# Copies and row scalings of layers 1 to 3 choose ScalarE or VectorE when the list scheduler places them

## The chip, the core and the metric

The kernel runs on one core of a Trainium2 chip. A core has five engines that run at the same time, each with its own in-order queue of instructions: TensorE (PE in the profile; its weight loads are a row of their own, PEld), VectorE (DVE), ScalarE (ACT), GpSimd (POOL) and SyncE (SP, which here issues the DMAs). They wait for each other through semaphores. Matrix products land in PSUM, a small memory of eight banks per core; GpSimd takes no part in reading it here, so whatever leaves PSUM is read by VectorE or ScalarE. The main memory on the chip is SBUF, 128 partitions wide.

The metric is the time of one execution in microseconds (us) on the device, as a median over runs.

## What is computed

Four layers in a row, with five attentions between them, over 32 sequences of 64 tokens with 256 features, and a context tensor of the same shape. All in fp32. Cut to its core:

```
x = x + Wo0 @ attn(norm(x), ctx)          # layer 0: 8 heads of 64, over channels
a = layernorm(ctx) * g + b                # layer 1: 16 heads of 16
x = x + tanh(gate) * attn(x Wq, a Wk, a Wv, mask) Wo
h = concat(ctx, x)                        # layer 2: queries from x, 128 keys
o = attn(x Wq, h Wk, h Wv, mask) Wo + x
x = x + gelu(rmsnorm(o) W1) W2            # with biases; hidden size 1024
x = x + attn(layernorm(x), itself) Wo     # layer 3, self-attention, mask applied to the scores
x = x + attn(layernorm(x), ctx) Wo        # layer 3, cross-attention
x = x + gelu(layernorm(x) W1) W2          # layer 3, MLP of 1024
```

"Layers 1 to 3" are all but the first, which holds an attention without the split into small heads. The code counts the attentions of layers 1 to 3 as `l` = 0 to 3: layer 1, layer 2, and the two of layer 3.

## The kernel before

**Tiling.** The 32 sequences make eight groups of four. A group's tokens are a tile of 128 partitions x 2 x 256 values (`xs[g]`). Attention goes in units: each unit is a pair of sequences with 16 heads of 64 keys (layer 2 takes two units a pair, with 8 heads of 128 keys each). The scores of a unit, 128 x 1024, fill one PSUM buffer (`s4`, a single one for the whole core). A unit then goes: maximum (DVE), subtraction (DVE, or POOL for every second masked unit), exponential (ACT), sum and reciprocal (DVE), scaling by POOL or a spread of the reciprocals to a row (`a_rows`, tile `rx`), two times four transposes on PE with a copy out of PSUM each (`a_turn`, tile `PTe`), 64-column products with the values (`a_values`), and a copy of the result (`a_fin`).

**Split precision.** Projections run as fp32r products of a high and a low part: `to_fm` transposes a tile, copies it to a rounded high part (`xTh...`), and subtracts that from the source for the low part (`xTl...`). So almost every projection waits for a copy and then for a subtraction. The same is done for the MLP's hidden tile (`u` to `xThh` and `xTlh`).

**Copies.** The operations that this case is about are these: the row scaling of the layer norms (`ln_apply`; its result is a tile in `boot`, scaled and shifted by two [128,1] columns `rstd` and `nmr`), the high part in `to_fm`, the evictions of queries and keys (`put`, tiles `qfm` and `kfm`, with or without a bias column), the values scattered into their places (`v_out`, `vbd`), `rx`, `PTe`, the attention result (`a_fin`: `rb`, `xTho`), the high part of the context (`split_`, `xTh<-boot`), and the high part of the MLP's hidden tile (`xThh<-u`). In the kernel before, all of them run on ScalarE, save a few value scatters on VectorE. The source lies in PSUM for most of them; `boot`, `rx`, `xTh<-boot`, `xThh` and `xTho<-rb` go from SBUF to SBUF.

**What sets the order.** Layer 0 (the first 440 us) is written out by hand; the weights' loading and the prologue of layer 1 are held in chains from which `fill` slips operations in. From `plan.on = True` (L1592) on, nothing is issued directly: every operation is recorded with a due time, and `Plan.go` (L246) orders the whole of layers 1 to 3. `link` finds the dependences from tiles and byte ranges; two engines in one PSUM bank are kept in order. `order` (L289) is a list scheduler: with a modelled time for each operation (`cost`, L194) it takes, again and again, the ready operation that can start earliest, on the engine that it is recorded for; among equals it takes the most urgent, by due time, less 3 for what drains PSUM, plus a random tie-breaker of up to 0.5 drawn from `SEED`. Each engine's queue then holds its instructions in just that order, and the slots of all tiles are chosen there too. All recorded operations carry one line in the profile, L125 (`write`); those of layer 0 carry L156 (`call`).

In `cost`, VectorE's time for a copy or a scaling from SBUF is 0.3 + 1.05e-3 us a column, from PSUM 0.14 + 1.05e-3; ScalarE's is 0.115 + 0.92e-3, 0.03 more from SBUF and 0.105 more for each [128,1] operand.

Of the kernel before, what the change touches and what calls it, by code (L numbers as in the profile page):

```python
# [20 lines left out]
D = 256  # L21
# [72 lines left out]
class Plan:  # L94
# [2 lines left out]


    RING = {"pj": 40}
    SEED, TIE = 4, 0.5  # L100

    def __init__(self, engines):
        self.engines = engines
# [12 lines left out]
    def shape(self, shape, dt):  # L116
        if self.scratch is None:
            import concourse.bacc as bacc
            self.scratch = bacc.Bacc("TRN2", target_bir_lowering=False, num_devices=1)
        self.n += 1  # L120
        return self.scratch.dram_tensor(f"s{self.n}", tuple(shape), dt, kind="ExternalInput").ap()

    def write(self, o):
        real = lambda x: x.real() if isinstance(x, View) else x
# [68 lines left out]

    def cost(self, o):  # L194

        outs, ins = o.outs, o.ins
        width = lambda x: max(1, self.size(x))
        w = width(outs[0])
        if o.key == "T":
            if o.method == "transpose":  # L200
                return 0.11, 0.25, (1, 1)
            l, r = ins[0], ins[1]
            k_, m_ = l.shape[0], self.size(l)
            rows = 4 if k_ <= 32 else 2 if k_ <= 64 else 1
            cols = 4 if m_ <= 32 else 2 if m_ <= 64 else 1
            n_ = self.size(r)
            if l.dtype == F32:
                return max(n_ * 1.67e-3, 0.1 if rows * cols == 1 else 0) / (rows * cols), 0.3, (rows, cols)
            return max(n_ * 0.418e-3, 0.12 if rows * cols == 1 else 0) / (rows * cols), 0.25, (rows, cols)
        if o.key == "S":  # L210
            return 0.64, 2.0, None
        w = max([w] + [width(x) for x in ins])
        out_of_banks = any(isinstance(x, View) and x.root.psum for x in ins)
        if o.key == "V":
            if o.method == "reciprocal":
                return 0.14 + w * 7e-3, 0.05, None
            if w <= 16:
                return 0.2, 0.05, None
            if out_of_banks or o.method in ("tensor_reduce", "bn_stats"):
                return 0.14 + w * 1.05e-3, 0.05, None  # L220
            return 0.3 + w * (1.05e-3 if o.method in ("tensor_copy", "tensor_scalar") else 1.3e-3), 0.05, None
        if o.key == "A":
            gelu = any(x == AF.Gelu_apprx_tanh for x in o.p)
            exp = any(x == AF.Exp or x == AF.Square for x in o.p)
            t = 0.115 + w * 0.92e-3 + 0.105 * len([x for n, x in o.k.items() if n in ("bias", "scale") and self.is_ap(x)])
            return t + (0 if out_of_banks or exp else 0.03), 0.1, "gelu" if gelu else "exp" if exp else None
        if o.method == "memset":
            return 0.1 + w * 0.85e-3, 0.05, None
        if w <= 16:
            return 0.75 if any(x == ALU.pow for x in o.p) else 0.3, 0.05, None  # L230
        three = len([x for x in ins if width(x) > 1]) > 1
        return 0.1 + w * (2.45e-3 if three and not self.repeats(ins[1]) else 1.95e-3), 0.05, None
# [21 lines left out]
    def link(self):  # L254
        atoms, seen = [], {}
        for i, o in enumerate(self.ops):
# [16 lines left out]
            for (name, rt, p0, p1, f0, f1), writes in places:  # L273
                if rt is not None and rt not in at.roots:
                    at.roots.append(rt)
                acc = seen.setdefault(name, [])
                for b, q0, q1, g0, g1, w in acc:
                    if b is at:
                        continue
                    bank = rt is not None and rt.psum and b.key != at.key  # L280
                    if bank or ((writes or w) and p0 < q1 and q0 < p1 and f0 < g1 and g0 < f1):
                        at.before[b] = True
                        b.after[at] = True
                if writes:
                    acc[:] = [x for x in acc if not (p0 <= x[1] and x[2] <= p1 and f0 <= x[3] and x[4] <= f1 and x[0] is not at and not (rt is not None and rt.psum))]
                acc.append((at, p0, p1, f0, f1, writes))
        return atoms

    def order(self, atoms):  # L289
# [25 lines left out]
        for at in atoms:  # L315
            at.wait = len(at.before)
            at.at = 0.0
            at.urgent = at.due + ties.uniform(0, self.TIE) - (3.0 if at.key in "VA" and any(isinstance(x, View) and x.root.psum for o in at.ops for x in o.ins) else 0.0)
            if not at.wait:
                ready[at.key].append(at)  # L320
        out = []

        def slots(at):
# [23 lines left out]
        while len(out) < n:  # L347
            best = None
            for e, rs in ready.items():
                cand = []  # L350
                for at in rs:
                    s = slots(at)
                    if s is None:
                        continue
                    t = max(free[e], at.at, s)
                    if at.form is not None and e == "A" and form.get(e) not in (None, at.form):
                        t += 0.4
                    cand.append((t, at))
                if not cand:
                    continue  # L360
                t0 = min(t for t, _ in cand)
                t, at = min(((t, at) for t, at in cand if t <= t0), key=lambda x: (x[1].urgent, x[1].index))
                if best is None or t < best[0]:
                    best = (t, at)
            if best is None:
                stuck = [(k, at.due, at.ops[0].method, [r.slot for r in at.takes]) for k, rs in ready.items() for at in rs]
                raise RuntimeError(f"no order: {len(out)} of {n}, {stuck[:20]}")
            t, at = best
            e = at.key
            ready[e].remove(at)  # L370
            d = at.time
            if at.form is not None:
                if form.get(e) not in (None, at.form):
                    d += 0.12 if e == "T" else 0.0
                    if e == "A":
                        t += 0.9
                form[e] = at.form
# [19 lines left out]
            for b in at.after:  # L397
                b.wait -= 1
                b.at = max(b.at, (t + d if b.key == e else end) + 0.06 * (b.key != e))
                if not b.wait:  # L400
                    ready[b.key].append(b)
            at.written = True
            out.append(at)
        self.atoms = out
# [4 lines left out]
def mk_kernel(ctx: ExitStack, tc: tile.TileContext, a: dict, out: bass.AP):  # L409
# [489 lines left out]
    def ln_apply(x, mv, rstd, tag):  # L899
        z = wt([P, 2, D], F32, "z", 2)  # L900
        nmr = wt([P, 2], F32, "nmr" + tag, 2)
        for i in range(2):
            G.tensor_scalar(nmr[:, i:i + 1], mv[:, i, 0:1], rstd[:, i:i + 1], -1.0, ALU.mult, ALU.mult)
            A.activation(z[:, i], x[:, i], AF.Identity, bias=nmr[:, i:i + 1], scale=rstd[:, i:i + 1])
        return z

    def to_fm(x, tag=""):
# [4 lines left out]
                T.transpose(p_[:, k * D + i * P:k * D + (i + 1) * P], x[:, i, k * P:(k + 1) * P], ident)  # L912
        hi, lo = fm_tiles(tag)
        hf, lf = hi.rearrange("p k t -> p (k t)"), lo.rearrange("p k t -> p (k t)")
        A.copy(hf, p_)
        V.tensor_tensor(lf, p_, f32(hf), ALU.subtract)
        return (hi, lo)

# [28 lines left out]
        return o  # L947

    def put(d, s_, bias):
        if bias is None:  # L950
            A.copy(d, s_)
        else:
            A.activation(d, s_, AF.Identity, bias=bias)

    def k_out(w, x, bias):

# [8 lines left out]
    def v_out(w, x, vb, vl, part=None):  # L965
# [3 lines left out]
        for b in range(2):  # L969
            for e in range(2):  # L970
# [3 lines left out]
                else:  # L974
                    dst = vb[e][part * 64:(part + 1) * 64]
                dst = dst.rearrange("p (i b) h d -> p i b h d", b=2)[:, :, b, :, e * 16:(e + 1) * 16]
                if vl == 1 and b == 0 and e == 0 or cur["boot"] and e == 0:
                    V.tensor_copy(dst, src)
                else:
                    A.copy(dst, src)  # L980

    def kbd_make(kt, kbs_, part=None):

# [75 lines left out]
    def a_rows(u):  # L1059
        u["rx"] = []  # L1060
        if u["kind"] != "k":
            rx = wt([P, 16, 16], F32, "rx", 2)
            sm = u["sm"].rearrange("p (r c h) -> p r c h", r=4, c=2).unsqueeze(4).broadcast_to([P, 4, 2, 2, 16])
            A.copy(rx.rearrange("p (c r h) d -> p r c h d", c=2, r=4), sm)
            rx = rx.rearrange("p (c h) d -> p c (h d)", c=2)
            u["rx"] = [rx[:, 0], rx[:, 1]]

    def a_turn(u, c):
# [1 line left out]
        for r in range(4):  # L1070
            T.transpose(pt[:, r * P:(r + 1) * P], u["e"][:, r, c * P:(c + 1) * P], ident)
        pe = wt([P, 4, P], F32, "PTe", 4)
        A.copy(pe.rearrange("p h q -> p (h q)"), pt)
        u.setdefault("pt", []).append(pe)

    def a_values(u):
# [12 lines left out]
    def a_fin(u):  # L1089
# [5 lines left out]
        hv, lv = [t[:, c, i * P:(i + 1) * P] for t in st["o"]]  # L1095
        ov = o_[:, 0:D].rearrange("p (c t) -> p c t", c=2)[:, c]
        if u["kind"] == "k":
            A.copy(hv, ov)
            V.tensor_tensor(lv, ov, f32(hv), ALU.subtract)
        else:  # L1100
            rb = wt([P, 2, P], F32, "rb", 2)
            A.copy(rb.rearrange("p c t -> p (c t)"), o_[:, D:2 * D])
            V.tensor_tensor(rb, ov, rb, ALU.mult)
            A.copy(hv, rb)
            G.tensor_tensor(lv, rb, f32(hv), ALU.subtract)

    def out_add(w, x, resid, dst):
# [121 lines left out]
    def ctx_steps(l, g, due, src=()):  # L1229
# [6 lines left out]

        def split_():
            hi, lo = fm_tiles()
            A.copy(hi, st["raw"])
            G.tensor_tensor(lo, st["raw"], f32(hi), ALU.subtract)  # L1240
            st["c"] = (hi, lo)
        step(n + "a", due - 2, fetch, *src)
# [36 lines left out]
    def mlp_steps(l, g, w, b1, row, key, dues, out_=None):  # L1279
# [3 lines left out]
        def up(j):  # L1283
# [7 lines left out]
                A.activation(t[:, c], p_[:, c * D:(c + 1) * D], AF.Gelu_apprx_tanh, bias=b1[:, j * 2 + c:j * 2 + c + 1])  # L1291
            st[f"h{j}"] = fm_tiles("h")
            hh, hl = st[f"h{j}"]
            A.copy(hh, t)
            V.tensor_tensor(hl, t, f32(hh), ALU.subtract)

        def down(j):
# [372 lines left out]
```

## Time and profile before

| | us |
|---|---|
| median of 3 runs | 1141.58 (1139.43 to 1143.37) |
| the profiled execution | 1139.34 |
| its span, first to last instruction | 1137.6 |
| PE busy in the span | 1064.6 |
| ACT busy | 909.2 |
| DVE busy | 861.2 |
| POOL busy | 783.1 |

A busy share is an average over stages that have different limits, so the stages are read one by one: layer 0 to about 440 us, a passage of some 25 us to the scheduled part, then layers 1, 2 and 3 in turn, overlapping by group. Idle time of an engine costs time only where another engine that sets the end waits for it. The span of a matrix instruction in the profile is modelled and overlaps with its neighbours, so that PE counts as busy somewhat beyond what it must do.

### The profile page before, as it was taken

What the parts mean: (1) busy time and instruction counts of PE and PEld (TensorE: products, weight loads), DVE (VectorE), ACT (ScalarE), POOL (GpSimd) and SP (SyncE); (2) the same over time, 40 slices, a digit from 0 to 9 for tenths busy, and PEclk for the clock granted to TensorE, in tenths of its full rate; (3) what the DMA queues carried; (4) which work ended last, traced back from release to release, by engine and by line L of the source; (5) the groups of instructions that cost most, each with busy time, mean ns of one, the idle gap of its engine ahead of it and who ended that gap; (6) DMA issues with size and microseconds to landing.
All of it is one profiled execution on the core that took longest, in us unless ns stands there. A gap on an engine that the chain in (4) does not pass through costs nothing.

```text
span 1137.6 us, 35727 instructions
## 1 busy us (share of the span) xinstructions
PE 1064.6 (94%) x14396; PEld 872.7 (77%) x14396; DVE 861.2 (76%) x1485; ACT 909.2 (80%) x2326; POOL 783.1 (69%) x919
## 2 busy tenths in 40 slices
PE   6999999999999996699999999999999989889998
PEld 4666666666666664588988989998998868779998
DVE  3778888787888872678788977777878888777842
ACT  2888888888888984477778888889898787878974
POOL 3789888888888864546545554457866999996520
PEclk9999999999999998799999999999999998989999
DMA  3001111111011000211211100001000111110000
GB/s 96 20 24 39 41 38 34 34 34 35 27 37 33 26 20 29 88 49 39 79 51 44 36 27 28 22 11 39 21 20 20 48 51 51 42 33 22 11 20 29
DMA packets 41301, 41.22 MB, mean 36 GB/s; under 512 B 7059, under 2 KB 37796, under 8 KB 41136
## 3 DMA queue, kind: packets, MB, share of 16 engines
q1 hardware_dynamic: 40816, 38.54, 10.9%
q8 instruction: 114, 1.87, 0.7%
q10 hardware_dynamic: 320, 0.40, 0.1%
q14 instruction: 51, 0.42, 0.1%
HBM read 26.30 MB, written 2.10 MB: 25 GB/s over the span
## 4 chain that ended last, share of the span: by engine, by line
PE 42%; POOL 8%; DVE 5%; ACT 2%; issue 1%; DVEq 0%; POOLq 0%; ACTq 0%
PE pj L125 39%; PE s L125 4%; POOL E L125 3%; DVE E L125 2%; DVE mx L125 1%; POOL xTlo L125 1%; POOL xTl L125 1%; ACT PTe L125 1%; DVE sm L125 1%; POOL boot L125 1%; POOL w L125 1%; POOL x L125 1%; POOL wraw L125 0%; ACT L125 0%; POOL rstda L125 0%
## 5 line engine op out<-in xcount | busy, mean ns | idle before, releaser
L156 POOL TENSOR_TENSOR E<-E,rs 128x512 f32<-128x512 f32 x256 | 263.2, 1042 | 51.7 <-DVE rs L156 46.7
L156 ACT ACTIVATE E<-sc,mx 128x256 f32<-128x256 f32 x512 | 237.9, 479 | 11.8 <-DVE rs L156 11.1
L156 DVE TENSOR_REDUCE mx<-sc 128x4 f32<-128x1024 f32 x128 | 156.3, 1221 | 6.6 <-PE sc L156 2.6
L156 PE MATMUL sc<-cd,T 64*128 64x256 f32 x1024 | 143.7, 400 | 11.7 <-ACT E L156 11.1
L125 POOL TENSOR_TENSOR E<-E,sm 128x512 f32<-128x512 f32 x96 | 101.2, 1079 | 68.5 <-DVE sm L125 55.8
L156 PE MATMUL av<-PT,us 128*64 128x256 f32 x1024 | 125.2, 385 | 0.3 <-DVE PT L156 0.3
L156 PEld LDWEIGHTS av<-PT,us 128*64 128x64 f32 x1024 | 68.1, 136 | 60.3 <-issue 21.0
L156 PEld LDWEIGHTS pt<-ident,E 64*128 64x128 f32 x2048 | 83.3, 139 | 37.4 <-POOL E L156 20.1
L156 PEld LDWEIGHTS sc<-cd,T 64*128 64x128 f32 x1024 | 89.2, 189 | 27.7 <-ACT E L156 19.8
L125 DVE TENSOR_REDUCE sm<-E 128x16 f32<-128x1024 f32 (+1 forms) x80 | 96.0, 1200 | 16.1 <-ACT E L125 16.0
L156 ACT ACTIVATION_READ_ACCUMULATOR E<-sc,mx 128x1 f32 x512 | 106.7, 208 | 0.0
L125 ACT COPY PTe<-pj 128x512 f32<-128x512 f32 x160 | 88.0, 590 | 17.7 <-PE pj L125 15.6
L125 PE MATMUL pj<-ident,E 128*128 128x128 f32 x640 | 90.3, 279 | 9.0 <-ACT E L125 3.2
L156 PE MATMUL pt<-ident,E 64*128 64x64 f32 x2048 | 94.7, 227 | 3.3 <-ACT PT L156 1.0
L125 PE MATMUL pj<-w,xThh 128*128 128x256 f32 x512 | 93.4, 287 | 0.1
L156 DVE COPY PT<-pt 128x512 f32<-128x512 f32 x128 | 86.7, 678 | 8.5 <-PE pt L156 7.8
L156 ACT COPY PT<-pt 128x512 f32<-128x512 f32 x128 | 75.3, 588 | 22.2 <-PE pt L156 21.0
L125 PE MATMUL pj<-xThn,w 128*128 128x256 f32 x512 | 92.3, 286 | 0.7 <-DVE rb L125 0.4
L156 DVE RECIPROCAL rs<-sm 128x2 f32<-128x2 f32 x256 | 40.7, 159 | 64.3 <-ACT E L156 60.1
L125 ACT ACTIVATE E<-E 128x1024 f32<-128x1024 f32 x80 | 84.9, 1062 | 5.4 <-DVE E L125 4.2
L125 PEld LDWEIGHTS pj<-ident,E 128*128 128x128 f32 x640 | 71.0, 142 | 17.7 <-ACT E L125 3.7
L125 DVE TENSOR_TENSOR xTlh<-u,xThh 128x512 fp32r<-128x512 f32 x64 | 54.2, 850 | 30.5 <-ACT xThh L125 30.2
(229 smaller groups left out, 2782.5 us busy)
## 6 DMA issues: line engine op xcount, KB each, us to landing
kb<-kfm SPq DMA_DIRECT2D x44, 128.0 KB, 2.0
xd<-in_x SPq DMA_DIRECT2D x32, 128.0 KB, 2.9
cd<-in_ctx SPq DMA_DIRECT2D x32, 128.0 KB, 2.7
boot<-in_ctxT SPq DMA_DIRECT2D x16, 256.0 KB, 2.9
kb<-kfm SPq DMA_DIRECT2D x64, 64.0 KB, 1.9
xt<-in_x SPq DMA_DIRECT2D x16, 128.0 KB, 2.0
boot<-in_ctx SPq DMA_DIRECT2D x8, 256.0 KB, 2.7
out<-x SPq DMA_DIRECT2D x8, 256.0 KB, 2.1
```

Source lines behind the costliest of these rows:

```text
L125: getattr(self.engines[o.key], o.method)(*[real(x) for x in o.p], **{k: real(x) for k, x in o.k.items()})
L156: return f(*p, **k)
```

## The change

A new method `Plan.either` records a copy, or a scaling by columns, under a key "F" instead of an engine. It holds two forms: an ACTIVATE for ScalarE (function Copy, or Identity with bias and scale) and a copy or a tensor-scalar instruction for VectorE. In `order` such an operation stands in the ready lists of both engines. VectorE may take it only where it could start there at least `WORTH` = 0.5 us sooner than on ScalarE by the scheduler's own times. When it is placed, it becomes that engine's form. Outside the scheduled part (the prologue) it always goes to ScalarE. ScalarE's form was a copy instruction before, and is an ACTIVATE with the function Copy after. Two "F" operations in one PSUM bank are kept in order of recording. The fixed rule that sent some value scatters of layer 2 to VectorE is gone, the one for the prologue stays. `SEED`, which draws the tie-breakers, goes from 4 to 3.

```diff
-    SEED, TIE = 4, 0.5
+    SEED, TIE = 3, 0.5
+    WORTH = 0.5
...
+    def either(self, d, src, bias=None, scale=1.0):
+
+        o = Op()
+        o.key, o.due, o.extra = "F", self.due, self.extra
+        self.extra = []
+        if bias is None:
+            o.method, o.p, o.k = "activation", (d, src, AF.Copy), dict(scale=scale)
+            o.other = ("tensor_copy", (d, src)) if scale == 1.0 else ("tensor_scalar", (d, src, scale, None, ALU.mult))
+        else:
+            o.method, o.p, o.k = "activation", (d, src, AF.Identity), dict(bias=bias, scale=scale)
+            o.other = ("tensor_scalar", (d, src, bias, None, ALU.add)) if isinstance(scale, float) else ("tensor_scalar", (d, src, scale, bias, ALU.mult, ALU.add))
+            assert not isinstance(scale, float) or scale == 1.0
+        if self.on:
+            self.ops.append(o)
+            return
+        o.key = "A"
...
@@ link
-                    bank = rt is not None and rt.psum and b.key != at.key
+                    bank = rt is not None and rt.psum and (b.key != at.key or at.key == "F")
@@ order
-                ready[at.key].append(at)
+                for e in "AV" if at.key == "F" else at.key:
+                    ready[e].append(at)
...
                     t = max(free[e], at.at, s)
+                    if at.key == "F" and e == "V" and max(free["A"], at.at, s) < t + self.WORTH:
+                        continue
...
+            if at.key == "F":
+                o = at.ops[0]
+                if e == "V":
+                    d = o.on_v
+                    o.method, o.p, o.k = *o.other, {}
+                o.key = e
...
@@ ln_apply
-            A.activation(z[:, i], x[:, i], AF.Identity, bias=nmr[:, i:i + 1], scale=rstd[:, i:i + 1])
+            plan.either(z[:, i], x[:, i], nmr[:, i:i + 1], rstd[:, i:i + 1])
@@ to_fm
-        A.copy(hf, p_)
+        plan.either(hf, p_)
@@ put
-        if bias is None:
-            A.copy(d, s_)
-        else:
-            A.activation(d, s_, AF.Identity, bias=bias)
+        plan.either(d, s_, bias)
@@ v_out
-                if vl == 1 and b == 0 and e == 0 or cur["boot"] and e == 0:
+                if cur["boot"] and e == 0:
                     V.tensor_copy(dst, src)
                 else:
-                    A.copy(dst, src)
+                    plan.either(dst, src)
@@ a_turn
-        A.copy(pe.rearrange("p h q -> p (h q)"), pt)
+        plan.either(pe.rearrange("p h q -> p (h q)"), pt)
@@ up (MLP)
-            A.copy(hh, t)
+            plan.either(hh, t)
...
```

The copies of `a_rows` (`rx`), of `a_fin` (`rb`, `xTho`) and of `split_` (`xTh<-boot`) are replaced in the same way.

More of the change, by code (lines that the diff above doesn't have):

```diff
@@ L121, in shape @@
         return self.scratch.dram_tensor(f"s{self.n}", tuple(shape), dt, kind="ExternalInput").ap()
+    def either(self, d, src, bias=None, scale=1.0):
[13 more added lines that the diff above has]
+        o.key = "A"
+        if self.chain is not None:
+            self.chain.append(o)
+        else:
+            self.write(o)
     def write(self, o):
@@ L194, in cost @@
     def cost(self, o):
+        if o.key == "F":
+            o.key = "V"
+            m, p, k = o.method, o.p, o.k
+            o.method, o.p, o.k = o.other[0], o.other[1], {}
+            o.on_v = self.cost(o)[0]
+            o.key, o.method, o.p, o.k = "A", m, p, k
+            t = self.cost(o)
+            o.key = "F"
+            return t
         outs, ins = o.outs, o.ins
@@ L317, in order @@
             at.at = 0.0
-            at.urgent = at.due + ties.uniform(0, self.TIE) - (3.0 if at.key in "VA" and any(isinstance(x, View) and x.root.psum for o in at.ops for x in o.ins) else 0.0)
+            at.urgent = at.due + ties.uniform(0, self.TIE) - (3.0 if at.key in "VAF" and any(isinstance(x, View) and x.root.psum for o in at.ops for x in o.ins) else 0.0)
             if not at.wait:
-                ready[at.key].append(at)
+                for e in "AV" if at.key == "F" else at.key:
+                    ready[e].append(at)
         out = []
@@ L364, in order @@
                     best = (t, at)
+                    at.engine = e
             if best is None:
@@ L368, in order @@
             t, at = best
-            e = at.key
-            ready[e].remove(at)
+            e = at.engine
+            for q in "AV" if at.key == "F" else at.key:
+                ready[q].remove(at)
             d = at.time
+            if at.key == "F":
[4 more added lines that the diff above has]
+                o.key = e
             if at.form is not None:
@@ L400, in order @@
                 if not b.wait:
-                    ready[b.key].append(b)
+                    for q in "AV" if b.key == "F" else b.key:
+                        ready[q].append(b)
             at.written = True
@@ L1063, in a_rows @@
             sm = u["sm"].rearrange("p (r c h) -> p r c h", r=4, c=2).unsqueeze(4).broadcast_to([P, 4, 2, 2, 16])
-            A.copy(rx.rearrange("p (c r h) d -> p r c h d", c=2, r=4), sm)
+            plan.either(rx.rearrange("p (c r h) d -> p r c h d", c=2, r=4), sm)
             rx = rx.rearrange("p (c h) d -> p c (h d)", c=2)
@@ L1097, in a_fin @@
         if u["kind"] == "k":
-            A.copy(hv, ov)
+            plan.either(hv, ov)
             V.tensor_tensor(lv, ov, f32(hv), ALU.subtract)
@@ L1101, in a_fin @@
             rb = wt([P, 2, P], F32, "rb", 2)
-            A.copy(rb.rearrange("p c t -> p (c t)"), o_[:, D:2 * D])
+            plan.either(rb.rearrange("p c t -> p (c t)"), o_[:, D:2 * D])
             V.tensor_tensor(rb, ov, rb, ALU.mult)
-            A.copy(hv, rb)
+            plan.either(hv, rb)
             G.tensor_tensor(lv, rb, f32(hv), ALU.subtract)
@@ L1238, in split_ @@
             hi, lo = fm_tiles()
-            A.copy(hi, st["raw"])
+            plan.either(hi, st["raw"])
             G.tensor_tensor(lo, st["raw"], f32(hi), ALU.subtract)
```

## The prediction

> **What bounds the kernel now.** I read the page's busy shares and slices first, then the windows, the waits of the matmul engine, and last the durations of the operations that change hands. The order list of both programs gave what moves.
>
> The page: TensorE is the busiest engine, and its row of slices shows where it is not full. (Rows: PE, the POOL engine, the granted clock; 28.4 us a digit.)
> ```profile
> PE 1064.6 (94%) x14396; PEld 872.7 (77%) x14396; DVE 861.2 (76%) x1485; ACT 909.2 (80%) x2326; POOL 783.1 (69%) x919
> ...
> PE   6999999999999996699999999999999989889998
> ...
> POOL 3789888888888864546545554457866999996520
> PEclk9999999999999998799999999999999998989999
> ```
> Layer 0 fills the first 440 us, and its order does not change. Then come two dips of PE: at 440 to 500 us, and at 900 to 1000 us. The windows give sizes (columns: PE, PEld, DVE, ACT, POOL busy us, then clock).
> ```profile
> 440.00:466.00 26.00, 12.73 (x111) 10.31 (x111) 5.57 (x15) 8.43 (x18) 11.34 (x17) 0.76 0.17 56
> 466.00:500.00 34.00, 30.57 (x487) 27.17 (x486) 25.01 (x36) 21.21 (x43) 14.74 (x21) 0.83 0.22 70
> ...
> 700.00:800.00 100.00, 99.51 (x1554) 90.44 (x1554) 76.27 (x118) 89.75 (x172) 60.12 (x69) 1.00 0.08 25
> 800.00:900.00 100.00, 96.61 (x1415) 88.23 (x1415) 80.88 (x114) 83.94 (x167) 74.62 (x62) 0.98 0.08 26
> 900.00:1000.00 100.00, 85.34 (x1228) 75.90 (x1227) 79.51 (x130) 81.84 (x172) 96.30 (x97) 0.93 0.15 49
> 1000.00:1100.00 100.00, 97.20 (x1247) 91.51 (x1247) 74.12 (x102) 83.98 (x160) 64.21 (x67) 0.98 0.06 19
> ```
> The 13.3 us of idle PE at 440 to 466 us are the prologue of layer 1, whose order is the same in both. From 466 us, where the scheduler rules, PE idles 3.4 us to 500; 2.7, 2.5, 0.5 and 3.4 us in the hundreds to 900; 14.7 us at 900 to 1000; 2.8 us to 1100; 4.2 us at the very end: 34 us in all. That is the whole stock a better order can draw on, apart from the clock. ACT is 90% busy at 700 to 800 us while PE idles 0.5 us: a full ScalarE is not by itself a loss here. At 900 to 1000 us POOL is the full engine (96.3 of 100), and no POOL instruction is touched.
>
> Who ended PE's waits from 466 us on (total us, times, longest):
> ```profile
> PE pj L125 <- ACT boot L125: 5.2, 7, 1.6
> PE pj L125 <- ACT PTe L125: 3.8, 6, 1.2
> PE pj L125 <- POOL xTl L125: 3.7, 3, 2.2
> PE pj L125 <- ACT E L125: 3.2, 2, 2.9
> PE pj L125 <- DVE rb L125: 2.9, 3, 1.3
> ```
> `boot` (the row scaling), PTe and the copy ahead of xTl and rb may now change engine; E (the exponential) may not.
>
> Prices (mean ns in the groups; min/median/max in the tile views):
> ```profile
> L125 ACT COPY PTe<-pj 128x512 f32<-128x512 f32 x160 | 88.0, 590 | 17.7 <-PE pj L125 15.6 <-ACT u L125 0.6
> L156 DVE COPY PT<-pt 128x512 f32<-128x512 f32 x128 | 86.7, 678 | 8.5 <-PE pt L156 7.8
> L125 ACT COPY rb<-pj 128x256 f32<-128x256 f32 x32 | 11.8, 372 | 8.3 <-PE pj L125 8.0
> L125 ACT ACT_TABLE_LOAD x45 | 57.7, 1283 | 1.2 <-DVE E L125 0.5
> ...
> L156 ACT ACTIVATE GT<-pt x1: 384/384/384, 10.0 to 10.0; 128x256 f32<-128x256 f32 x1
> ...
> L125 DVE TENSOR_SCALAR boot<-boot,rrms x16: 317/347/1375, 611.5 to 835.1; 128x256 f32<-128x256 f32 x16
> ...
> L125 DVE TENSOR_TENSOR xTlh<-u,xThh x64: 637/692/2280, 622.2 to 1131.6; 128x512 fp32r<-128x512 f32 x64
> ```
> Rows that move from PSUM cost 0.09 us more on DVE than on ACT (678 against 590). Rows inside SBUF are another matter: the DVE scaling takes 347 ns, but where a POOL instruction runs through it, 994 to 1375 ns; the two-input subtraction 692 ns, and up to 2280. ACT's SBUF copies show no such tail (622 ns mean).
>
> **The change, part by part.** In the changed program 83 of these operations stand on DVE, where 16 did (DVE 1487 to 1554 instructions). From PSUM, 55: 16 of 512 columns at 0.68 us, 3 of 256 at 0.41, 8 of 128 at 0.28, 17 with a bias at about 0.47 (the 512-column DVE form with a bias takes 0.73, less 256 columns at 0.27), 11 value scatters at 0.41, less the 16 before: 10.9 + 1.2 + 2.2 + 8.0 - 2.1 = 20 us. Inside SBUF, 28: 14 of 256 columns at 0.35 to 1.38, 14 of 512 at 0.35 to 2.28 (this form has no row: the 256-column scaling bounds it from below, the blocked two-input row from above; nearest is the unblocked 0.69): 10 to 51 us, 15 by the nearest rows. DVE grows by 30 to 71 us, ACT sheds 35 us and two table loads (2 x 1.28). Neither bounds a stage, so the gain lies in what PE waits for:
>
> - *900 to 1000 us: -4.* POOL's work is the same, its place is not. I added up, in both orders, the POOL durations queued ahead of each matmul that needs a POOL result, and set against it the PE work ahead of it (start to start 119 ns for 256 columns and 109 for 128, the medians of this trace). POOL's lead climbs from 170.8 us near matmul 8,100 to 210.2 at 9,535 before, from 170.7 to 205.8 after: 4.3 us less. Bounds: 0 (the lead was covered anyway) and -14.7 (all the idle).
> - *466 to 900 and after 1000 us: -3.* PE idles 15.3 us there. Direct waits for movable ACT operations add up to 10.3 us over the whole stage (5.2 + 3.8 + 1.3 for vbd), about half of them outside the 900s; with DVE as second server I take three fifths of 5. Bounds 0 and -8.
> - *First units, 466 to 490 us: +1.* The old order has PE turn the next group's rows while the first softmax runs; the new one goes straight to the first E transposes, behind DVE's third maximum and subtraction (2 x 1.22), a reciprocal (0.25) and POOL's scaling (1.08): 3.8 us of PE waiting, near 4.4 with the score matmul ahead. The old order stalls 3.1 us there. Bounds -3 and +4.4.
> - *DVE copies inside SBUF that meet POOL: +1.* Behind such a copy DVE's in-order queue waits, with the next unit's maximum, which frees the only score buffer. Seven of the 28 stand between matmuls 8,394 and 9,370 (895 to 1005 us), three of them together at 9,340. All blocked, they lose 5 x 1.03 + 2 x 1.59 = 8.3 us. DVE has 20% to spare there, so I take +1; bounds 0 and +8.
> - *Clock: -2.* The granted clock is 0.93 at 900 to 1000 us, 7 us of PE time; the halved spells come after PE's pauses, so I scale with the stalls. Bounds -7 and +5.
> - *Other form of the copy on ACT: 0.* The 553 copies that stay become ACTIVATEs: 384 ns (the GT row) against 372, 12 ns each, 6.6 us in all, in ACT's spare 14 to 20%. If a copy stands in front of PE it shows: at most +1. The prologue's vbd, boot and bootx copies change form only: 0.2 us.
> - *Queues:* SP keeps 293 issues and POOL 924 instructions; some weight loads and mask loads are issued a place earlier or later. DMA is under 20% busy in every window after 500 us; 0, and if a load were late, 2 to 3 us (its landing time) once. The added rule that two such copies of one PSUM bank are ordered costs nothing where both stay on ACT, which is in order already.
>
> Sum: -4 - 3 + 1 + 1 - 2 = -7 on the profiled execution, 1139.34 us with a span of 1137.6: 1132.3. That execution is 2.24 us under the median of 1141.58, so I forecast 1134.6.
>
> **Two rules weighed.** The trace's row first: the DVE scaling at 347 ns alone, up to 1375 beside POOL. The Trainium skill (GPSIMD Engine Reference, section Key points) says that POOL shares its SBUF interfaces with VectorE, and contends with VectorE instructions in a two-port mode or with two SBUF inputs. It agrees with both tails, and speaks against the 28 SBUF moves: were each of them to hold up POOL or DVE on the path, the sum would turn from -7 to about 0 by the 8.3 us in the POOL stretch alone. It gives no reason against the 55 moves from PSUM. The Trainium skill (ScalarE: Activation LUTs, section What ACT_TABLE_LOAD costs) puts a switch of tables at 1283 ns and a drain of about 1380: by it two fewer loads free 5.3 us of ACT, by the row 2.6; with ACT off the path the sum is the same.
>
> **The rivals.**
> *Nothing to be seen, 1140.* The 900s are POOL's own work, and elsewhere PE idles 15 us of 500. For it: PE at 99.5% beside ACT at 90%. Against it: boot and PTe head PE's waits. The sum keeps only a part of the second item: 1141.6 - 2.
> *Slower, 1151.* The SBUF copies on DVE run into POOL. Excess 8.3 us in the POOL stretch; the other 21 lose 9 x 1.03 + 12 x 1.59 = 28 us if blocked, POOL is busy some 57% there: 16, and a third on the path: 5. With the second item's -3: +10. It decides from 7 us on the path (gain gone); beyond 10.4 us it is slower. For it: 2280 ns tails; a scheduler that prices such a copy by width alone sees nothing of them. Against it: DVE has a fifth of spare time.
> *The change does little:* 83 of some 800 either-way operations use DVE, and the matmul order keeps its shape; this falls under the first rival.
>
> **How the numbers follow.** The sum's case 0.48, with its own range 1127 to 1138 (-14 to -3.4); no difference 0.22; slower 0.30. Within 0.3% (3.4 us, about what a measurement of this kernel can tell from none) I put 0.24, for the edge of the first case; faster 0.46, slower 0.30. The range reaches 1125 below (-16.6, the first two items at three quarters of their bounds) and 1153 above (the slower rival and 2 us).
>
> **What would show it.** Right: PE idle in the 900s near 10 us instead of 14.7, clock there above 0.93; waits of PE for ACT boot and PTe halved; DVE 895 to 930 us busy, ACT 870 to 885; copies as ACTIVATE near 600 ns. Wrong: DVE copies xThh, boot or rx over 1 us with PE waiting behind them; new PE waits for DVE; half-clock spells outside 440 to 490 and the 900s.

## The result, and the profile after

The changed kernel takes 1148.28 us as a median of 7 runs (1145.43 to 1150.43), against 1141.58 for the kernel before (7 runs too): a ratio of 1.0059, 95% interval 1.0044 to 1.0074. It is slower by 0.6%; 1134.6 was forecast, with the slower side at 0.30. The profiled execution took 1149.95 us with a span of 1148.2.

The page of the changed kernel (same rows as before: PE, POOL, granted clock):
```profile
PE 1065.0 (93%) x14396; PEld 874.6 (76%) x14396; DVE 916.8 (80%) x1552; ACT 887.2 (77%) x2257; POOL 786.1 (68%) x919
...
PE   6999999999999995799999999999989978889998
...
POOL 3789888889888763555556454467784999998520
PEclk9999999999999998699999999999999999999999
```
PE's busy time is the same within 0.4 us; the span grew by 10.6 us, nearly all of it PE idle (span less busy: 73.0 before, 83.2 after). The two profiled executions lie 2.2 us under and 1.7 us over their kernels' medians, so 6.7 of the 10.6 us belong to the change. ACT lost 22 us of work, DVE gained 56. The windows of the changed kernel say where (columns PE, PEld, DVE, ACT, POOL busy, clock):
```profile
440.00:466.00 26.00, 13.57 (x67) 11.14 (x65) 4.94 (x12) 8.48 (x18) 11.38 (x17) 0.66 0.13 41
466.00:500.00 34.00, 28.27 (x510) 24.70 (x510) 25.98 (x37) 19.23 (x37) 15.52 (x22) 0.80 0.25 74
...
700.00:800.00 100.00, 98.15 (x1505) 91.28 (x1504) 84.05 (x130) 83.82 (x160) 61.66 (x72) 1.00 0.09 28
800.00:900.00 100.00, 90.80 (x1297) 82.38 (x1295) 89.81 (x117) 75.78 (x143) 64.92 (x55) 0.97 0.05 19
900.00:1000.00 100.00, 85.12 (x1371) 74.75 (x1374) 92.66 (x138) 76.37 (x158) 96.83 (x88) 0.95 0.17 53
1000.00:1100.00 100.00, 95.73 (x1204) 89.58 (x1203) 88.62 (x124) 81.67 (x154) 73.26 (x76) 0.98 0.07 22
```
PE idles 5.7 us at 466 to 500 (3.4 before), 9.2 at 800 to 900 (3.4), 14.9 at 900 to 1000 (14.7), 4.3 to 1100 (2.8). DVE, which was 74 to 81% busy from 800 us on, is now 89 to 93% busy, while ACT has fallen to 76 to 82%. What PE waited for from 466 us on:
```profile
PE pj L147 <- ACT E L147: 10.7, 6, 3.4
PE pj L147 <- DVE xTlh L147: 6.2, 5, 2.2
PE pj L147 <- ACT PTe L147: 5.3, 8, 1.2
PE pj L147 <- POOL E L147: 4.8, 1, 4.8
```
ScalarE's row scaling, which headed the list before with 5.2 us, has fallen to 0.5. New are DVE's low part of the MLP (xTlh, no wait before) and a threefold wait for the exponential. That wait lies wholly in the stretch of 900 to 1000 us, whose own view begins like this before and after:
```profile
PE pj L125 <- ACT boot L125: 3.9, 5, 1.6
PE pj L125 <- POOL xTl L125: 3.7, 3, 2.2
PE pj L125 <- ACT E L125: 3.2, 2, 2.9
...
PE pj L147 <- ACT E L147: 10.7, 6, 3.4
PE pj L147 <- POOL xTl L147: 1.6, 2, 1.0
```
In the longest of these waits (3.4 us, to 929.91) ScalarE starts the exponential at 928.80, 0.03 us after GpSimd has subtracted the maximum:
```profile
926.87 1.90 POOL L147 TENSOR_TENSOR E<-E,mx 128x1024 f32<-128x1024 f32 x1
```
The groups of DVE that bear on the change:
```profile
L147 DVE TENSOR_TENSOR xTlh<-u,xThh 128x512 fp32r<-128x512 f32 x64 | 61.7, 969 | 22.2 <-ACT xThh L147 21.9
L147 DVE TENSOR_SCALAR boot<-boot,rrms 128x256 f32<-128x256 f32 x16 | 12.5, 807 | 0.0
L147 DVE CAST xThh<-u 128x512 fp32r<-128x512 f32 x13 | 12.1, 934 | 7.0 <-ACT u L147 5.8 <-PE pj L147 1.2
L147 DVE TENSOR_SCALAR boot<-x,rstda,nmra 128x256 f32<-128x256 f32 x5 | 6.6, 1343 | 0.0
L147 DVE COPY rx<-sm 128x256 f32<-128x256 f32 x4 | 5.4, 1360 | 0.1
L147 DVE CAST xTho<-rb 128x256 fp32r<-128x256 f32 x3 | 4.5, 1499 | 0.1
L147 DVE COPY PTe<-pj 128x512 f32<-128x512 f32 x8 | 5.4, 678 | 0.4 <-PE pj L147 0.3
```
The copies from PSUM cost what the forecast took (PTe 678 ns). Those inside SBUF shown here average 0.9 to 1.5 us, where ACT takes 0.4 to 0.63 for the same. (`boot<-boot,rrms` and xTlh stood on DVE before.) The stretch of DVE's queue that ends in one of PE's waits (timeline of DVE; start us, us):
```profile
853.39 1.31 DVE L147 TENSOR_SCALAR boot<-x,rstda,nmra 128x256 f32<-128x256 f32 x1
854.72 1.22 DVE L147 TENSOR_TENSOR E<-s,m 128x1024 f32<-128x1024 f32 x1
855.86 0.41 DVE L147 TENSOR_TENSOR rb<-pj,rb 128x256 f32<-128x256 f32 x1
856.31 2.29 DVE L147 CAST xTho<-rb 128x256 fp32r<-128x256 f32 x1
858.52 1.21 DVE L147 TENSOR_TENSOR E<-s,m 128x1024 f32<-128x1024 f32 x1
859.65 0.41 DVE L147 CAST xThh<-u 128x512 fp32r<-128x512 f32 x1
859.99 0.41 DVE L147 TENSOR_TENSOR rb<-pj,rb 128x256 f32<-128x256 f32 x1
860.32 2.52 DVE L147 TENSOR_TENSOR xTlh<-u,xThh 128x512 fp32r<-128x512 f32 x1
```
and POOL in the same time:
```profile
853.26 1.28 POOL L147 TENSOR_TENSOR w<-boot,w 128x512 fp32r<-128x512 f32 x1
...
856.07 2.38 POOL L147 TENSOR_TENSOR E<-E,c 128x1024 f32<-128x1024 f32 x1
```
The scaling (853.39 to 854.70) and the copy to xTho (856.31 to 858.60) each end 0.15 us after the POOL instruction that ran when they started (854.54 and 858.45). DVE has no gap in this stretch; the copy that takes 0.28 us alone holds the queue for 2.29. The last, xTlh, has two SBUF inputs and meets POOL as it did before the change; pushed back to 860.32, it comes 1.7 us late for PE.

### The profile page after: what moved, and what is told of

Same layout as the page of the kernel before. It is cut to its first block, busy times and chain, and to the rows that moved or that the text cites. A ratio compares the mean times of both kernels' runs of the same rounds, so it can differ in the third digit from the quotient of the medians.

```text
span 1148.2 us, 35768 instructions
## 1 busy us (share of the span) xinstructions
PE 1065.0 (93%) x14396; PEld 874.6 (76%) x14396; DVE 916.8 (80%) x1552; ACT 887.2 (77%) x2257; POOL 786.1 (68%) x919
## 4 chain that ended last, share of the span: by engine, by line
PE 37%; POOL 9%; DVE 9%; ACT 3%; issue 2%; ACTq 0%; POOLq 0%; DVEq 0%
PE pj L147 33%; POOL E L147 4%; PE s L147 3%; DVE E L147 2%; DVE sm L147 1%; DVE mx L147 1%; DVE xTlh L147 1%; DVE boot L147 1%; POOL xTl L147 1%; POOL xTlo L147 1%; POOL rstda L147 1%; DVE xThh L147 1%; ACT L147 1%; ACT E L147 1%; ACT vbd L147 0%
## 5 line engine op out<-in xcount | busy, mean ns | idle before, releaser
L147 PE MATMUL pj<-ident,E 128*128 128x128 f32 x640 | 93.6, 287 | 23.0 <-ACT E L147 10.7
L147 PEld LDWEIGHTS pj<-ident,E 128*128 128x128 f32 x640 | 73.9, 147 | 32.6 <-ACT E L147 12.0
L147 ACT ACTIVATE PTe<-pj 128x512 f32<-128x512 f32 x152 | 84.7, 596 | 15.7 <-PE pj L147 13.6
L147 DVE TENSOR_TENSOR xTlh<-u,xThh 128x512 fp32r<-128x512 f32 x64 | 61.7, 969 | 22.2 <-ACT xThh L147 21.9
```

What stands on the lines that cost most here:

```text
L147: getattr(self.engines[o.key], o.method)(*[real(x) for x in o.p], **{k: real(x) for k, x in o.k.items()})
```

## The experiments

Four theories. A: the 28 copies and scalings from SBUF to SBUF that now stand on VectorE run into GpSimd and hold up VectorE's queue. B: the order as a whole is worse, because it was drawn anew. C: ScalarE's ACTIVATE costs more than its copy instruction. Later came three on the scheduler itself. D: it charges the wait for another engine (an engine crossing) ahead of every operation whose engine is still open. E: ScalarE has too much without the 16 value scatters that a fixed rule sent to VectorE. F: the end of that rule is what costs. Ratios are to the kernel before on the same chip, with 95% intervals.

**The 28 back on ScalarE, in the same order.** The scheduler still places them for VectorE, and every tile slot and place stays; only the queue that they are issued to differs.
```diff
                 if e == "V":
                     d = o.on_v
+                    if not any(isinstance(x, View) and x.root.psum for x in o.ins):
+                        o.back = o.method, o.p, o.k
...
             for o in a_.ops:
+                if hasattr(o, "back"):
+                    o.key, (o.method, o.p, o.k) = "A", o.back
                 self.write(o)
```


> The changed kernel in its own order and with its own tile slots, but the 28 operations from SBUF to SBUF that the scheduler gave to VectorE are issued on ScalarE at the same place of the order. Theory A (those 28 meet GpSimd in SBUF, run 0.9 to 1.5 us instead of 0.35 to 0.7 and hold up VectorE's queue): the time falls by at least 5 us, from 1148 to 1143 or less, and VectorE is busy 30 us less (917 to about 887). Theory B (the order itself became worse, by the new draw of the tie-breakers and the new places): the time stays within 3 us of 1148 or rises, since the order is the same. Theory C (ScalarE's form of the copy): no change.

1141.56 us, ratio 1.0003 (0.9993 to 1.0014). The whole loss of the kernel as given is gone. The page of that kernel:
```profile
PE 1060.8 (93%) x14396; PEld 870.2 (76%) x14396; DVE 892.5 (78%) x1524; ACT 897.2 (79%) x2285; POOL 785.0 (69%) x919
```
two of its windows, with 6.1 us of PE idle at 800 to 900 us in place of 9.2, and 14.6 at 900 to 1000 in place of 14.9:
```profile
800.00:900.00 100.00, 93.93 (x1403) 85.62 (x1403) 86.32 (x117) 81.51 (x158) 71.90 (x61) 1.00 0.06 22
900.00:1000.00 100.00, 85.42 (x1351) 75.24 (x1350) 91.14 (x140) 79.58 (x165) 97.06 (x93) 0.97 0.16 50
```
and two of its PE waits from 466 us on, which stood at 10.7 and 6.2, with the group of xTlh, which stood at 969 ns:
```profile
PE pj L147 <- ACT E L147: 12.3, 6, 3.9
...
PE pj L147 <- DVE xTlh L147: 3.6, 5, 1.8
...
L147 DVE TENSOR_TENSOR xTlh<-u,xThh 128x512 fp32r<-128x512 f32 x64 | 62.3, 979 | 41.2 <-ACT xThh L147 41.2
```
So neither the wait for the exponential nor the length of xTlh belongs to the loss: both are as high here (xTlh took 850 ns on average before the change). What fell is PE's wait for xTlh, by 2.6 us: the queue ahead of it is shorter. In the stretch shown above DVE now has four gaps, 1.25, 0.52, 0.60 and 0.46 us, and PE waits 0.95 us for the same xTlh instead of 1.69, though it takes 2.57 us itself.

DVE is busy 24 us less for 28 instructions, 0.87 us each. Of the 6.7 us of span regained, 2.5 are PE idle and 4.2 PE busy: by the records of the granted clock it stood at half for 51.2 us of the span in the changed kernel and for 45.6 here (45.7 before). PE's pauses and the clock's halving fell together.

**The same 28 put on VectorE in the order before.** The kernel before, unchanged but for the queue of the same 28 recorded operations.
```diff
+        ON_V = [2761, 3035, ...
...
             for o in a_.ops:
+                if ids[id(o)] in ON_V:
...
+                    o.key = "V"
...
                 self.write(o)
```
(Cut: the list holds the 28, and the lines left out give them VectorE's form.)

> The kernel before in its own order and slots, but the same 28 recorded operations from SBUF to SBUF that the changed kernel put on VectorE are issued there, at their places in the old order. Theory A: slower by 4 to 10 us, 1146 to 1152, VectorE busy some 30 us more, the 28 averaging over 0.9 us. Theory B: within 3 us of 1141.6.

1142.18 us, ratio 1.0017 (1.0009 to 1.0026). Slower, but by 1.9 us, less than expected. The groups of that kernel:
```profile
L125 DVE CAST xThh<-u 128x512 fp32r<-128x512 f32 x13 | 9.9, 760 | 2.0 <-PE pj L125 1.9
L125 DVE TENSOR_SCALAR boot<-x,rstda,nmra 128x256 f32<-128x256 f32 x5 | 2.8, 579 | 0.0
L125 DVE COPY rx<-sm 128x256 f32<-128x256 f32 x4 | 1.8, 438 | 0.0
L125 DVE CAST xTho<-rb 128x256 fp32r<-128x256 f32 x3 | 0.9, 285 | 0.0
```
In these places six of the 28 wait for a GpSimd instruction (take over 0.1 us more than unhindered); in the changed kernel sixteen do. Summed over the 28, and less what they take unhindered (0.42 us for xThh, 0.40 for boot and xTh, 0.30 for rx, 0.28 for xTho), they lose 5.9 us here and 19.3 in the changed kernel. The time lost is 1.9 and 6.7 us: in both about a third. So theory A holds in kind, and its price depends on where the order puts the copies. The 11 us of VectorE time that the 28 take here even unhindered cost at most those 1.9 us, so in that order a fuller VectorE by itself costs little.

**ScalarE's form.** The same order, with plain copies as copy instructions again.
```diff
+        if o.key == "A" and o.method == "activation" and o.p[2] == AF.Copy and o.k.get("scale") == 1.0:
+            o.method, o.p, o.k = "copy", o.p[:2], {}
```


> The changed kernel in the same order, but every plain copy on ScalarE is a copy instruction again instead of an ACTIVATE with the function Copy. Theory C (the other form costs the 7 us): 553 copies give back 10 to 12 ns each, ScalarE is busy some 6 us less, and the time falls by up to 6 us. Theories A and B: ScalarE is not what bounds a stage, so less than 2 us.

1149.28 us, ratio 1.0073 (1.0057 to 1.0090): no gain, theory C is out. It is also a second reading of the changed kernel's order, on the same chip as the first experiment: 7.7 us above it.

**The draw.** Theory B was tried by drawing the tie-breakers from other numbers, in both kernels (the edit of the first of six).
```diff
-    SEED, TIE = 4, 0.5
+    SEED, TIE = 3, 0.5
```


> The kernel before with the tie-breakers drawn from 3 instead of 4, nothing else. Theory B (the draw matters as much as the change): the time moves by 3 us or more, to 1145 or above if this draw is a bad one. Theory A: within 3 us of 1141.6.

> The changed kernel with the tie-breakers drawn from 4 as before. Theory B: the time comes back to 1143 or less. Theory A: it still has SBUF copies on VectorE beside GpSimd and stays at 1145 to 1151; VectorE's scalings and copies from SBUF average over 0.9 us again.

> The kernel before with draw 1. Theory B: 1145 or above, and with draw 2 the four draws spread by 5 us or more, so that draw 4 was a good one. Theory F: 1139 to 1145, as with draws 3 and 4.

> The kernel before with draw 2. As for draw 1: Theory B 1145 or above, Theory F 1139 to 1145.

> The changed kernel with draw 1 (the kernel before with it: 1147.5). Theory B alone (only the draw matters): on either side of 1147.5, anywhere in 1140 to 1158. Theories A and B together: 4 to 7 us above what the order would take without SBUF copies on VectorE, so above 1148 more likely than not.

> The changed kernel with draw 2 (the kernel before with it: 1153.6). Theory B alone: 1140 to 1158, and below 1153.6 more likely than not, since that draw was a bad one. If the changed kernel is slower in three or four of the four pairs, it is worse beyond its draw; if in two, nothing is shown beyond the SBUF copies.

| draw | kernel before, us (ratio) | changed kernel, us (ratio) | difference, % |
|---|---|---|---|
| 4 | 1141.58 (1) | 1155.88 (1.0130) | 1.30 |
| 3 | 1143.79 (1.0022) | 1148.28 (1.0059) | 0.37 |
| 1 | 1147.50 (1.0057) | 1161.75 (1.0173) | 1.16 |
| 2 | 1153.56 (1.0109) | 1159.60 (1.0163) | 0.54 |

The draw alone moves the kernel before by 1.09%, more than the 0.59% of the change as given, and each kernel as it stands has the best of its four draws. On each of the four draws the changed kernel is slower, by 0.84% on average. The SBUF copies do not explain the four differences: on draw 4 they lose 4.4 us by the sum above (25 of them), on draw 1 12.4 (31), on draw 2 16.6 (41), on draw 3 19.3 (28), and the smallest of these sums goes with the largest difference.

**PSUM sources alone may choose**, the order made anew, with both draws.
```diff
-        o.key, o.due, o.extra = "F", self.due, self.extra
+        o.key, o.due, o.extra = "F" if isinstance(src, View) and src.root.psum else "A", self.due, self.extra
```


> The changed kernel, but only operations that read PSUM may choose; those from SBUF to SBUF are recorded for ScalarE, and the order is made anew. Theory A: all of the loss goes, 1136 to 1142, and VectorE's two-input subtraction for the MLP's low part is back at 0.85 us or less on average. Theory B: anywhere between 1136 and 1150, since the order is new.

> The same with the draw of the kernel before. Theory A: 1136 to 1142 again. Theory B: several us away from the run with draw 3; the distance between the two is a measure of what a draw is worth.

1149.61 (ratio 1.0094) and 1152.47 us (1.0107). Theory A alone had 1136 to 1142: it falls as the whole story. Nor did xTlh come back to the 850 ns that it named (919 on draw 3). Without SBUF copies on VectorE a new order is no better.

**The scheduler's treatment of the key.** First VectorE was forbidden by the threshold:
```diff
-    WORTH = 0.5
+    WORTH = 1e9
```


> The changed kernel with the threshold at 1e9 instead of 0.5 us: no either-way operation goes to VectorE, nor the 16 value scatters that a fixed rule sent there. What is left of the change is the ACTIVATE form, the order rule within a PSUM bank and the new draw. Theory A: close to the kernel before, 1139 to 1145. Theory B: as far off as the draw alone (the kernel before with draw 3).

1160.29 us (1.0174; 1.0151 to 1.0198), where the kernel before with the same draw took 1.0022. What PE waited for most there is PTe, 14.1 us in 17 waits. Theories D and E were made for this. Four kernels try them, in this order: all recorded for ScalarE from the start; the crossing charged by engine (the repair); the repair with 0.8 us added to the scheduler's price of an SBUF copy on VectorE; and the repair with VectorE forbidden by the threshold as above. The edits, cut: the first two lines are the first kernel's, the last two the third's, those between the repair.
```diff
-        o.key, o.due, o.extra = "F", self.due, self.extra
+        o.key, o.due, o.extra = "A", self.due, self.extra
...
-                    t = max(free[e], at.at, s)
+                    t = max(free[e], at.on[e] if at.key == "F" else at.at, s)
...
+                for q in b.on:
+                    b.on[q] = max(b.on[q], (t + d if q == e else end) + 0.06 * (q != e))
...
-            o.on_v = self.cost(o)[0]
+            o.on_v = self.cost(o)[0] + (0.0 if any(isinstance(x, View) and x.root.psum for x in o.ins) else 0.8)
```


> The changed kernel with every either-way operation recorded for ScalarE from the start, draw 3: what is left of the change is the ACTIVATE form and the end of the fixed rule for 16 value scatters; the scheduler's treatment of the key F is gone. The run where VectorE was merely forbidden took 1160. Theory D (the scheduler adds an engine crossing, 0.1 to 0.16 us, ahead of each F operation even where its producer is on the same engine, and so spaces ScalarE's work badly): this run comes back to 1141 to 1147, near the kernel before with draw 3 (1143.8). Theory E (ScalarE simply has too much without the 16 scatters on VectorE): it stays at 1155 or above.

> The changed kernel with one repair in the scheduler: for an F operation it keeps the earliest start on each engine by itself, so that on its producer's own engine no crossing is charged. Theory D: faster than the changed kernel by 5 us or more, at or under 1143, although SBUF copies still go to VectorE. Theory A alone: within 3 us of 1148.

> The repair, and 0.8 us added to the scheduler's price of an F operation from SBUF on VectorE, about what the blocked ones lost on average in the changed kernel. Theories A and D together: the fastest so far, 1132 to 1139, with fewer SBUF copies on VectorE than 28. If neither matters to the sum, 1140 to 1150 by the draw.

> The repair with VectorE forbidden (threshold 1e9), draw 3. Against the run that forbade VectorE without the repair (1160): Theory D: 1141 to 1148, near the run recorded for ScalarE. If it stays near 1160, the order rule for two F operations in one PSUM bank is what costs, not the crossing.

1154.42 (1.0119), 1153.18 (1.0114), 1156.79 (1.0148) and 1153.20 us (1.0106). Theory D falls: the repair does not make the changed kernel faster (1148.28 without it), and without the key the time is not that of the kernel before. Only where VectorE is forbidden did the repair gain, from 1.0174 to 1.0106, about the time of the kernel recorded for ScalarE. Theory E had 1155 or above for that kernel, and it took 1154.42: neither theory's range holds it. The price does not help either: 26 SBUF copies still go to VectorE (24 with the repair alone). It could hardly keep them away, since the scheduler chooses by the start on each engine, and the price enters only how long VectorE is then taken to be busy.

**The fixed rule** for 16 value scatters was taken from the kernel before, and given back to the changed one.
```diff
-                if vl == 1 and b == 0 and e == 0 or cur["boot"] and e == 0:
+                if cur["boot"] and e == 0:
```


> The kernel before without its fixed rule: the 16 value scatters of layer 2 that stood on VectorE go to ScalarE, nothing else (draw 4, new order). Theory F (the end of this rule costs some 10 us): 1149 or above. Theory B (the draw spreads the orders by several us either way): anywhere from 1138 to 1158, no nearer to one end.

> The changed kernel with the fixed rule kept (16 value scatters on VectorE whatever the scheduler finds), draw 3. Theory F: faster than 1148 by 3 us or more. Theory A: the SBUF copies on VectorE go on costing, 1145 to 1150.

1149.38 us (1.0083; 1.0069 to 1.0097) without it, and 1153.01 (1.0110; 1.0093 to 1.0128) with it. The end of the rule costs the kernel before 0.8%, and its return costs the changed one 0.5%. There is a second reading of the end of the rule: since `cost` prices both forms of a copy on ScalarE alike, the kernel recorded for ScalarE is, for the scheduler, the kernel before without the rule on draw 3, and it took 1.0119 against 1.0022 with the rule. So on two draws the end of the rule costs the kernel before 0.8 and 1.0%, but its return to the changed kernel does not pay. Each of these is within the spread of the draws: theory F is not shown.

What stays open: why the changed scheduler's orders are slower on all four draws; the end of the fixed rule is one candidate that is not ruled out. That the loss of the kernel as given lies in 28 copies is shown, in its own order; that such copies make every order of this scheduler slower is not.

## Why the prediction was wrong, point by point

Two steps failed. The sum took the gain of a better order for granted (-8 us without the item on the copies inside SBUF), and it took those copies at +1. The first experiment parts the two: the changed order with the 28 copies on ScalarE takes 1.0003 of the kernel before, so the order brought nothing of the 8; and the 28 copies cost 6.7 us instead of 1.

- **DVE copies inside SBUF, +1: mis-sized, 6.7 us measured in the order as given.** The term looked at seven copies in one stretch and put the other 21 at nothing, without a reason. In VectorE's queue the seven lost 6.1 us, of a bound of 8.3; the other 21 lost 13.2 (at 635, 751, 817 to 856, 1028, 1062 and 1080 to 1086 us). "DVE has 20% to spare, so +1" failed too: spare time on average does not help an in-order queue in a stretch where it has no gap. The slower rival named the mechanism and the scheduler's blindness, and counted all 28: 8.3 us for the seven, and 16 us for the rest with a third on the path. That third was a guess that came out: about a third of all that was lost is what the time shows (6.7 of 19.3, 1.9 of 5.9). One price was too high: the 512-column copy takes 0.42 us unhindered, where the nearest row gave 0.69.
- **900 to 1000 us, -4: not there.** PE idles 14.9 us instead of the 10 forecast. The waits that the text named did shrink: PE's direct waits for POOL there from 5.0 to 1.6 us, those for the row scaling from 3.9 to nothing. In their place PE waits 10.7 us for the exponential, 3.2 before. So the gain that was counted from POOL's lead did not become time: PE waits for POOL through ScalarE as well (the longest of these waits, shown above), and POOL is 96.8% busy there as before (96.3). DVE went from 79.5 to 92.7% busy in that stretch, but PE idled as long with DVE at 79.5%, and no run isolates its part. The copies inside SBUF are not the reason, since the first experiment idles 14.6 us there.
- **466 to 900 and after 1000 us, -3: other waits came.** Outside the 900s, PE's waits for ScalarE's row scaling fell from 1.3 to 0.5 us and that for vbd (1.3) went, but those for PTe rose from 2.6 to 5.3 and those for DVE's xTlh from nothing to 6.2. PE idle in these windows: 15.3 to 25.8 us, and 24.3 in the first experiment. What failed is "DVE as second server": no wait for DVE was set against the waits that it would take over.
- **First units, +1: right in kind.** PE waits 4.8 us for POOL's first E, where the text worked out 3.8 to 4.4; the window's idle time grew by 2.3.
- **Other form of the copy, 0: right.** PTe went from 590 to 596 ns on ACT, and the old form in the new order gained nothing. ScalarE ended at 887.2 us busy, just over the 870 to 885 named.
- **Clock, -2: wrong in sign.** 51.2 us at half clock against 45.7, in more spells; the text had scaled it with PE's stalls, and these grew.
- **Queues, 0: right as far as PE's waits show.** No DMA is among them from 466 us on.
- **What the sum left out:** the order's own spread. Four draws of the kernel before spread by 12 us. A forecast of -7 for a change that makes the order anew, against a kernel on its best of four draws, needed a term for that. On the same draw the kernel before took 1.0022; whether 2 of the 7 us go with the draw is not shown, since the changed order without the 28 copies took 1.0003.

The signs of being wrong that the text gave were the right ones, and they came: boot and rx on DVE over 1 us on average, new waits of PE for DVE, and half-clock spells at 845, 865 and 1029 us.

## What to carry to other kernels

Before a copy or scaling is moved to VectorE, ask where its operands lie: from PSUM it cost what the row said, inside SBUF it waited out GpSimd's wide two-input instructions, and everything behind it in VectorE's queue waited with it. A scheduler that knows such a copy by its width alone cannot see this: sixteen of the 28 that it placed here had to wait. Where a change makes a list scheduler's order anew, measure a few draws of both kernels first: here the draw moved the time by 1.1%, and a single pair of kernels could not have told the change from it. And count what a moved operation costs wherever it stands, not only in the stretch that one hopes to shorten.

## What the runs showed of the hardware

A VectorE copy or scaling between SBUF tiles that starts while GpSimd runs a tensor-tensor instruction of 256 columns or more (0.7 to 2.4 us) ends, in nearly all cases, a fixed time after GpSimd's end: 0.15 us for 256 columns and 0.28 us for 512. Of the 28 in the changed kernel ten took over a microsecond, up to 2.63, where the copy also waited out a memset that followed on GpSimd:
```profile
816.97 2.63 DVE L147 CAST xThh<-u 128x512 fp32r<-128x512 f32 x1 [1.16 <-PE pj L147]
...
816.03 2.39 POOL L147 TENSOR_TENSOR E<-E,c 128x1024 f32<-128x1024 f32 x1
818.37 0.95 POOL L147 MEMSET vbd<- 128x1024 f32 x1
```
The copy ends at 819.60, the memset at 819.32. Narrow GpSimd instructions did not hold them: under its scalings of 1 to 64 columns (nmrm, ck), with up to 0.46 us still to run, the same copies took 0.37 to 0.45 us, as alone, and in the changed kernel on draw 4 a row scaling that began under a two-column tensor-tensor instruction of 1.0 us took 0.40. The Trainium skill (GPSIMD Engine Reference, section Key points) speaks of contention between the two engines; the runs show for these forms that it is a full wait and not a slower rate. Unhindered, VectorE is the faster engine for them: 0.42 us for 128 x 512 to fp32r, against 0.62 on ScalarE.
